# A fused chain of RNN, scan, LSTM and adapted layer: a shorter lead of the RNN, another slot plan, and the input bias on VectorE

## The chip, the cores and the metric

The kernel runs on one core of a Trainium2 chip. The metric is the device time of one execution in microseconds (us), lower is better; the time of a kernel is the median of its runs. A profiled execution has a time of its own, which is given beside its span.

## What is computed

Four layers follow one another, each added to its input. The sequence is 1024 steps long, the batch 4, the width 512; everything is in 32-bit floats. `cond` is one vector per batch row.

```python
# L0, an RNN, started from h0 = cond
next_h = jnp.tanh(x_t @ Wx + b + prev_h @ Wh)
# L1, taps that come from cond, two projections, a linear scan
proj = conv @ Wp + bp;  b_t = softplus(proj[..., :64]);  c_t = tanh(proj[..., 64:]);  u = x @ Ws + bs
state = decay * state + dt * b_t * u_t;   y_t = c_t * state;   out = y @ Wo + bo
# L2, an LSTM, started from h0 = cond, c0 = 0; gates i, f, o (sigmoid) and g (tanh)
A = x_t @ Wx + b + prev_h @ Wh
next_c = f * prev_c + i * g;   next_h = o * jnp.tanh(next_c)
# L3, a weight per batch row, made from cond: layernorm, w1, gelu, w2, then a rank-8 product
layer = base_layer[None] + jnp.einsum('bdr,bkr->bdk', x_a, x_b);   out = einsum('btc,bco->bto', x, layer)
```

L0 and L2 are recurrences: step t needs step t-1 whole. L3's weight depends on `cond` alone, so it is made once.

## The kernel before

**Tiling.** Everything is kept transposed: 128 partitions hold a quarter of the width, 4 such quarters lie side by side, then time, then batch. Time is cut into 32 chunks of 32 steps. Products are cut into four column tiles of 32, which run beside one another on TensorE.

**Stages.** `do_pass(c)` (L712) runs 32 steps. In each step t it issues one LSTM step of chunk c, one RNN step of chunk c+2, and whatever *jobs* stand in that slot: the scan layer of chunk c+1 (`ssm_jobs`, L416), the adapted layer of chunk c-1 (`adapt_jobs`, L661), the RNN's input projection of chunk c+3 (`project0`, L292), the LSTM's input projection of chunk c+1 (`input_jobs`, L689) and its bias (`late_jobs`, L705). So the RNN leads the LSTM by two chunks, 64 steps. Passes -2 and -1 have RNN steps and no LSTM; in passes 30 and 31 the RNN is over.

**Order.** The order is written out by hand; each engine does its instructions in the order of issue. A job is a triple: slot t, a place, and the function. Place "pe" comes after the LSTM's matmuls and ahead of the RNN's; "gap" comes on VectorE and ScalarE after half B's cell and ahead of its h; "end" comes after the RNN's tanh. Within one slot and place the jobs go in the order of the list: adapt, scan, x load, RNN projection, input projection, bias.

**An LSTM step.** The width is dealt with in two halves, A and B, so that one's elementwise work lies beside the other's matmuls. `lstm_mm` (L350) issues 96 matmuls (the state is carried in three 16-bit parts): A with the state of half A, part of B, A with half B's state, the rest of B. Then for each half: a 32 x 32 block transposition out of PSUM (L377), a sum over the parts and the input (L382), the tanh of all gates (L389), products (L393), cell (L398), tanh (L403), h (L406) and two subtractions that split h (L187). The next step's first matmul waits for half A's second split; its half-B matmuls wait for half B's. The input, `xw2`, is copied in by ScalarE one step ahead (`lstm_input`, L366).

**An RNN step.** 32 matmuls (L335), a transposition (L343), a sum (L344), a tanh (L347).

**Input projection.** For each group of 8 steps: four jobs of 8 matmul records (`input_mm`, L316), two transpositions out of PSUM (`input_turn`, L320), then the bias and a scale of 0.5 for three gates, by ScalarE, 32 calls per chunk (`input_bias`, L328). All four groups of chunk c+1 are projected in slots 15 to 30 of pass c.

**Set-up.** `early` (L629) holds functions for given steps of passes -2 to 0, issued after the "end" jobs: the split of the LSTM's weights into 16-bit parts (`split_wh2`, 16 blocks, 3 in 2 of each 3 steps from step 4), the decay, the fold of the convolution's bias (`fold_conv`), centring and norm of `cond` (`adapt_center`, `adapt_norm`), `adapt_hidden`, then 32 blocks of w2 (`adapt_w2`, one per step from slot 3 of pass -1, so 29 in pass -1 and 3 in pass 0), `adapt_gather`, `adapt_sum`, and 16 blocks of the weight (`adapt_layer`, slots 8 to 30 of pass 0). w2 comes in 32 loads of 512 KB through four buffers that reuse the place of the weight; load j+4 is issued by `adapt_w2(j)` (L581, L583). `base_identity` (L618) adds the identity.

**Slots in a steady pass.** RNN projection 0, 10, 11, 12; taps 1 to 4 and the skip product 5; adapted layer's sums 2 to 5, products 6 to 9; elementwise work of the scan layer 4 to 12; its output product 13; input projection 15 to 30; x load (four DMAs of 64 KB on SyncE) 2. No slot has two PE jobs.

Of the kernel before, what the change touches and what calls it, by code (L numbers as in the profile page):

```python
# [14 lines left out]
P = 128  # L15
# [5 lines left out]
TG = 8  # L21
CT = 32
# [15 lines left out]
def cond_resid_kernel(ctx: ExitStack, tc: tile.TileContext, a: dict, out: bass.AP):  # L38

# [135 lines left out]
    def load_late():  # L175
        quads(nc.sync, w1, a["w1"].rearrange("(j c q) n -> j q c n", j=4, c=KC))
        for j in range(W2_BUFS):
            load_w2(j)
        quads(nc.sync, base, a["base"].rearrange("(j c q) n -> j q c n", j=4, c=KC))
# [63 lines left out]
    def prepare_decay():  # L243
        for f in softplus_parts(sp, vec[:NS, 2:4], 2, "p"):
            f()
        nc.vector.tensor_mul(dec1, sp[:, 0:1], dt)
        nc.vector.tensor_scalar(dec1, dec1, -1.0, 1.0, ALU.mult, ALU.add)
        nc.vector.tensor_copy(decay, dec1.to_broadcast([NS, TC]))
# [12 lines left out]
    b2s = const.tile([P, 4, KC], F32, name="b2s", tag="b2s")  # L261

    def scale_b2():
        nc.vector.tensor_scalar(b2s[:, 0:3], b2[:, 0:3], 0.5, None, ALU.mult)
        nc.vector.tensor_copy(b2s[:, 3], b2[:, 3])

    def split_wh2(k, g):

        w, scale, cols = layer[:, k, g], 0.5 if g == 3 else 0.25, slice(g * D, (g + 1) * D)
# [55 lines left out]
    def input_bias(c, n, g, m):  # L325

        x = xw2[c % 2][:, g, m, TG * n : TG * (n + 2), :]
        nc.scalar.activation(x, x, AF.Identity, bias=b2s[:, g, m : m + 1], scale=1.0 if g == 3 else 0.5)  # L328
# [39 lines left out]
    class Half:  # L368
# [19 lines left out]
        def gates(self):  # L388
            nc.scalar.activation(self.gc[:, :4], self.gc[:, :4], AF.Tanh)  # L389
# [26 lines left out]
    def ssm_jobs(c):  # L416
# [3 lines left out]
        def sm(name):  # L420
            return small.tile([NS, TOK], F32, name=name, tag=name, bufs=1)

        jobs = [
            (m // 2, ("gap", "end")[m % 2], lambda m=m: v.tensor_add(x1[:, m, 3:, :], x[:, m], h[:, m]))
            for m in range(KC)
# [22 lines left out]
        jobs += [(1 + k, "pe", lambda k=k: taps(k)) for k in range(KC)]  # L448
        jobs.append((5, "pe", skip))

        def turn(n):
# [5 lines left out]
            (4, "end", lambda: act.activation(z, pb[:NS, 0, :], AF.Identity, bias=vec[:NS, 0:1])),  # L457
            (4, "end", lambda: act.activation(e, pb[:NS, 0, :], AF.Abs, bias=vec[:NS, 0:1])),
            (5, "end", lambda: act.activation(e, e, AF.Exp, scale=-1.0)),
            (5, "end", lambda: act.activation(u, e, AF.Copy, bias=2.0)),  # L460
            (6, "end", lambda: act.activation(cg, pb[NS:, 0, :], AF.Tanh, bias=vec[NS:, 0:1])),
            (7, "end", lambda: v.tensor_mul(u, u, e)),
            (7, "end", lambda: v.tensor_mul(w, u, u)),
            (7, "end", lambda: act.activation(p, w, AF.Copy, scale=2.0 * SERIES[-1])),
            (12, "end", lambda: act.copy(s1, y_last)),
# [17 lines left out]
        jobs += [(6 + n // 3, place(n), lambda n=n: turn(n)) for n in range(4)]  # L483
        jobs += [(8 + n // 3, place(n), f) for n, f in enumerate(chain)]
# [6 lines left out]
        def x2_end(m):  # L491
# [6 lines left out]
            (13, "pe", out_mm),  # L498
            *((13 + m // 2, "end", lambda m=m: x2_end(m)) for m in range(KC)),
            (14, "end", lambda: act.copy(x1[:, :, 0:3, :], x1[:, :, TC : TC + 3, :])),  # L500
# [4 lines left out]
    hid = prep.tile([P, KC, B], F32, name="hid", tag="hid")  # L505
# [45 lines left out]
    def adapt_hidden():  # L551
# [12 lines left out]
        nc.vector.tensor_add(hid, tt[:, :, :B], bm1.unsqueeze(2).to_broadcast([P, KC, B]))  # L564
        nc.scalar.activation(hid, hid, AF.Gelu)

    def adapt_w2(j):
# [4 lines left out]
        for k in range(KC):  # L572
            for t in range(4):
                n0 = P // 2 * (t % 2)
                nc.tensor.matmul(  # L575
                    ps[CT * t : CT * t + B, :], hid[:, k, :], w2[j][:, t // 2, k, n0 : n0 + P // 2],
                    start=(k == 0), stop=(k == KC - 1),
                )
        for t in range(4):
            copy = (nc.vector.tensor_copy, nc.scalar.copy)[t % 2]  # L580
            copy(xr[CT * t : CT * t + B, half, hd, rg], ps[CT * t : CT * t + B, :])  # L581
# [36 lines left out]
    def base_identity():  # L618
# [11 lines left out]
    early = {  # L630
        (-2, 9): [prepare_decay], (-2, 12): [scale_b2], (-2, 24): [fold_conv], (-2, 26): [adapt_center], (-2, 28): [adapt_norm],
        (-1, 2): [adapt_hidden], (-1, 20): [base_identity],
    }
# [3 lines left out]

    late = None
    for n in range(4 * KC):
        first, second = split_wh2((1, 0, 2, 3)[n // 4], n % 4)  # L640
        t = 4 + 3 * n // 2
        if late:
            at(-2, t, late)
        at(-2, t, first)
        late = second
    at(-2, 29, late)
    at(-2, 30, load_late)

    for half in range(2):
        at(-1, half, lambda half=half: adapt_bias(half))  # L650
        at(0, 7, lambda half=half: adapt_sum(half))
    for j in range(NW2):
        c, t = divmod(3 + j, TC)
        at(c - 1, t, lambda j=j: adapt_w2(j))
        if j % (NW2 // 2) == NW2 // 2 - 1:
            at(c - 1, t, lambda half=j // (NW2 // 2): adapt_gather(half))
    for n in range(B * KC):
        at(0, 8 + 3 * n // 2, lambda n=n: adapt_layer(n // KC, n % KC))
# [200 lines left out]
```

## Time and profile before

| | |
|---|---|
| median of 3 runs | 4811.99 us (4811.18 to 4814.89) |
| profiled execution: time, span | 4806.8 us, 4805.0 us |
| first LSTM transposition (L377) | 192.4 us |
| pass 0, from its first LSTM transposition to the next pass's | 162.9 us |
| a pass of 2 to 29, mean of the same | 143.3 us |
| pass 30, the RNN over | 142.5 us |
| TensorE's granted clock, mean | 0.993 |
| TensorE at half clock | 29.9 to 36.7, 43.6 to 50.4, 57.2 to 111.8 us |

How it is read. The page gives for each engine the busy time, its share of the span and the number of instructions; PE is the matmuls, PEld the weight loads, DVE VectorE, ACT ScalarE, POOL GpSimd, SP SyncE. A matmul's record is 0.27 us long while the next one starts some hundredth of a us later, so a matmul group's worth is read from start to start. The chain is the work that ended last, followed back from the end, with each engine's and line's share of the span. In a table of stretches each row has the stretch (us from the start), its length, then the busy time and instructions of PE, PEld, DVE, ACT and POOL, then the granted clock, DMA's share and GB/s. In a timeline each row has the start, the time to the end of the last of the merged instructions, the engine, the line, the operation, what it writes and reads, shapes, how many, and in brackets the idle time before it and what ended it.

### The profile page before, as it was taken

To read this page: it belongs to the slowest core of one execution; us is meant where nothing else is said; L and a number is where in the kernel's file an instruction comes from. 1 tells how busy PE (TensorE), PEld (TensorE's weight loads), DVE (VectorE), ACT (ScalarE), POOL (GpSimd) and SP (SyncE) were. 2 spreads that over 40 slices of the span, in tenths; PEclk is the share of its full clock that TensorE was granted. 3 is DMA by queue.
4 is the path that set the end of the run, shared out by engine and by line. 5 is a ranking of instruction groups with operands and counts; after the bars stand their busy time and mean duration, and the time that the engine had idled before them with its cause. 6 is when DMAs were issued, how large, how long until landed. Compare 5 with 4: busy or idle time off the path is not lost.

```text
span 4805.0 us, 321617 instructions
## 1 busy us (share of the span) xinstructions
PE 4609.9 (96%) x147040; PEld 3529.9 (73%) x147040; DVE 3816.7 (79%) x17843; ACT 1749.1 (36%) x8712; POOL 52.1 (1%) x95
## 2 busy tenths in 40 slices
PE   6899999999999999999999999999999999999876
PEld 4777777777777777777777777777777777777654
DVE  3678888888888888888888888888888878888776
ACT  2333333333333333333333333333333333333332
POOL 2100000000000000000000000000000000000000
PEclk7999999999999999999999999999999999999999
DMA  6400000000000000000000000000000000000000
GB/s 138 130 4 9 9 9 9 7 7 9 9 9 9 7 8 7 9 9 9 7 9 7 9 9 9 7 9 6 9 9 9 9 7 6 9 7 6 6 3 7
DMA packets 38787, 67.47 MB, mean 14 GB/s; under 512 B 9056, under 2 KB 26080, under 8 KB 36400
## 3 DMA queue, kind: packets, MB, share of 16 engines
q1 hardware_dynamic: 34064, 46.68, 3.8%
q8 instruction: 1149, 18.83, 1.7%
q14 instruction: 214, 1.75, 0.1%
q0 software_dynamic: 2208, 0.19, 0.1%
q10 hardware_dynamic: 1152, 0.01, 0.0%
HBM read 38.34 MB, written 8.39 MB: 10 GB/s over the span
## 4 chain that ended last, share of the span: by engine, by line
PE 94%; DVE 5%; issue 1%; ACT 0%; DMA 0%; ACTq 0%; DVEq 0%; SPq 0%
PE acc L360 58%; PE acc L335 18%; PE proj L316 9%; PE pb L290 3%; PE proj L290 2%; PE ada L673 2%; DVE tt L377 1%; DVE gc L382 1%; DVE h L187 1%; PE ssm_out L290 1%; DVE h L406 1%; DVE prod L393 0%; DVE gc L398 0%; PE pl L615 0%; PE pp L575 0%
## 5 line engine op out<-in xcount | busy, mean ns | idle before, releaser
L360 PE MATMUL acc<-wh,h 128*12 128x256 bf16 x98304 | 2875.0, 273 | 134.7 <-DVE h L187 130.0
L360 PEld LDWEIGHTS <-h 128*12 128x12 bf16 x98304 | 2266.7, 87 | 693.9 <-DVE h L187 372.3
L377 DVE STREAM_TRANSPOSE tt<-acc 128x256 f32<-128x256 f32 x2048 | 922.0, 450 | 425.5 <-PE acc L360 305.6
L335 PEld LDWEIGHTS acc<-wh,h 128*4 128x4 f32 x32768 | 815.6, 88 | 521.3 <-issue 212.2
L335 PE MATMUL acc<-wh,h 128*4 128x128 f32 x32768 | 1109.1, 276 | 31.6 <-ACT h L347 27.8
L389 ACT ACTIVATE gc<-gc 128x32 f32<-128x32 f32 x2048 | 469.7, 229 | 1038.6 <-DVE gc L382 948.4
L382 DVE TENSOR_REDUCE gc<-tt 128x32 f32<-128x128 f32 x2048 | 777.1, 379 | 35.3
L187 DVE TENSOR_TENSOR h<-h 128x8 f32<-128x8 f32 (+1 forms) x4098 | 681.1, 166 | 104.7
L403 ACT ACTIVATE th<-gc 128x8 f32<-128x8 f32 x2048 | 427.2, 209 | 831.9 <-DVE gc L398 831.9
L347 ACT ACTIVATE h<-pre 128x16 f32<-128x16 f32 x1024 | 221.4, 216 | 1144.7 <-DVE pre L344 1144.7
L316 PE MATMUL proj<-wx,x 128*32 128x512 f32 x4096 | 529.5, 592 | 2.6 <-issue 1.5
L406 DVE SCALAR_TENSOR_TENSOR h<-gc,th 128x8 f32<-128x8 f32 x2048 | 343.1, 168 | 221.8 <-ACT th L403 205.1
L343 DVE STREAM_TRANSPOSE tt<-acc 128x128 f32<-128x128 f32 x1024 | 316.2, 309 | 70.3 <-PE acc L335 70.1
L398 DVE SCALAR_TENSOR_TENSOR gc<-prod 128x8 f32<-128x8 f32 x2048 | 341.9, 167 | 35.5
L366 ACT COPY tt<-xw 128x32 f32<-128x32 f32 x2048 | 327.9, 207 | 0.0
L393 DVE SCALAR_TENSOR_TENSOR prod<-gc 128x16 f32<-128x16 f32 x2048 | 315.3, 154 | 0.0
L328 ACT ACTIVATE xw<-xw,b2s 128x64 f32<-128x64 f32 x1024 | 293.6, 334 | 0.4
L344 DVE TENSOR_TENSOR pre<-xw,tt 128x16 f32<-128x16 f32 x1024 | 179.8, 176 | 37.4
L290 PE MATMUL proj<-xin,wx 128*32 128x128 f32 x4096 | 138.8, 278 | 11.9 <-DMA wx<-in_Wx_dram 11.8
L290 PE MATMUL pb<-x,wp 128*32 128x128 f32 x4096 | 139.5, 274 | 0.1
L673 PE MATMUL ada<-layer,x 128*32 128x512 f32 x1024 | 131.6, 592 | 3.0 <-DVE x L666 3.0
L290 PEld LDWEIGHTS proj<-xin,wx 128*32 128x32 f32 x4096 | 117.1, 112 | 14.0 <-DMA wh<-in_Wh_dram 11.8
(116 smaller groups left out, 1179.0 us busy)
## 6 DMA issues: line engine op xcount, KB each, us to landing
layer<-in_w2T_dram SPq DMA_DIRECT2D x32, 512.0 KB, 4.1
xin<-in_xT_dram SPq DMA_DIRECT2D x128, 64.0 KB, 2.1
out_dram<-x SPq DMA_DIRECT2D x128, 64.0 KB, 1.8
layer<-in_Wh_dram SPq DMA_DIRECT2D x16, 256.0 KB, 9.7
wx<-in_Wx_dram SPq DMA_DIRECT2D x4, 1024.0 KB, 15.5
wx<-in_Wx_dram SPq DMA_DIRECT2D x4, 256.0 KB, 5.2
wh<-in_Wh_dram SPq DMA_DIRECT2D x4, 256.0 KB, 7.9
layer<-in_w_dram SPq DMA_DIRECT2D x4, 256.0 KB, 23.7
```

The costliest lines, as they stand in the source:

```text
L187: nc.vector.tensor_tensor(h[:, :, n], h[:, :, n - 1], upper(h[:, :, n - 1]), ALU.subtract)
L290: nc.tensor.matmul(dst[CT * j : CT * (j + 1)], columns(j), x, start=first, stop=final)
L316: nc.tensor.matmul(ps[CT * j : CT * (j + 1), :], tok, w[:, j], start=(k == 0), stop=(k == KC - 1))
L335: nc.tensor.matmul(acc0[CT * j : CT * j + B, :], h[:, k, (t - 1) % TC, :], wh0[:, k, j * P : (j + 1) * P], start=(k == 0), stop=(k == KC - 1),
L360: nc.tensor.matmul(acc2[mh][CT * j : CT * j + NP * B, :], parts, w[:, :, n0 : n0 + 2 * CT], start=(k == 0 and n == 0), stop=(k == KC - 1 a ...
L366: nc.scalar.copy(tt2[m][t % 2][:, :, :, :B], xw2[c % 2][:, :, 2 * m : 2 * m + 2, t, :])
L377: nc.vector.transpose(self.tt[:, :, :, B:].rearrange("p g c b -> p (g c) b"), acc2[self.m])
L382: nc.vector.tensor_reduce(self.gc[:, :4].rearrange("p g c b -> p (g c) b"), self.tt[:, :, :, : (1 + NP) * B].rearrange("p g c (s b) -> p ( ...
L389: nc.scalar.activation(self.gc[:, :4], self.gc[:, :4], AF.Tanh)
L398: nc.vector.scalar_tensor_tensor(self.c, self.prod[:, 1], 0.5, self.prod[:, 0], ALU.mult, ALU.add)
L403: nc.scalar.activation(self.th, self.c, AF.Tanh, scale=0.5)
L406: nc.vector.scalar_tensor_tensor(self.out[:, :, 0], self.gc[:, 2], 1.0, self.th, ALU.add, ALU.mult)
```

## The change

The RNN leads by `LEAD` = 52 steps. In pass c and slot t the RNN's step is chunk and step `divmod(c * 32 + t + 52, 32)`; pass -2 starts at slot 12. So chunk c+1's RNN output is complete after slot 11, and the scan layer moves from slots 0 to 14 to slots 9 to 26. Of the LSTM's input projection only the first 8 steps of chunk c+1 are made in pass c (slots 25 to 30); the other three groups are made in the pass that uses them, from slots 0, 4 and 8. One of a group's two transpositions moves from "end" to "gap". The bias is one VectorE addition for two gates (eight per chunk), half of them in an "end" and half in a "gap"; it no longer scales. In its place the weights and the bias of gate g are doubled once and the gates' tanh has a scale of 0.5. The sum of x and h is three VectorE calls, the last on the last four steps. The set-up is numbered by RNN steps: one weight split per step from step 5, w2 blocks from step 32, two in three steps, 12 before the LSTM's first step and 20 in pass 0, each with 32 weight columns in place of 4 and one ScalarE copy in place of four copies; the sums and the identity at steps 23 and 24 of pass 0, the weight's blocks from slot 25 of pass 0 to slot 8 of pass 1, and the adapted layer's products at slots 16 and 21 to 23.

```diff
+LEAD = TC + 20
...
+    def double_g(k):
+        w = wx2[:, k, 3 * D :]
+        nc.scalar.activation(w, w, AF.Copy, scale=2.0)
...
-        w, scale, cols = layer[:, k, g], 0.5 if g == 3 else 0.25, slice(g * D, (g + 1) * D)
+        w, scale, cols = layer[:, k, g], 1.0 if g == 3 else 0.5, slice(g * D, (g + 1) * D)
...
-    def input_bias(c, n, g, m):
-
-        x = xw2[c % 2][:, g, m, TG * n : TG * (n + 2), :]
-        nc.scalar.activation(x, x, AF.Identity, bias=b2s[:, g, m : m + 1], scale=1.0 if g == 3 else 0.5)
+    def input_bias(c, n, g):
+
+        x = xw2[c % 2][:, g : g + 2, :, TG * n : TG * (n + 1), :].rearrange("p g c t b -> p g c (t b)")
+        nc.vector.tensor_add(x, x, b2[:, g : g + 2].unsqueeze(3).to_broadcast([P, 2, KC, TG * B]))
...
-            nc.scalar.activation(self.gc[:, :4], self.gc[:, :4], AF.Tanh)
+            nc.scalar.activation(self.gc[:, :4], self.gc[:, :4], AF.Tanh, scale=0.5)
...
         jobs = [
-            (m // 2, ("gap", "end")[m % 2], lambda m=m: v.tensor_add(x1[:, m, 3:, :], x[:, m], h[:, m]))
-            for m in range(KC)
+            (9, "end", lambda: add(slice(0, 2), 0, TC - 4)),
+            (10, "gap", lambda: add(slice(2, 4), 0, TC - 4)),
+            (11, "end", lambda: add(slice(0, 4), TC - 4, TC)),
         ]
...
-        jobs += [(1 + k, "pe", lambda k=k: taps(k)) for k in range(KC)]
-        jobs.append((5, "pe", skip))
+        jobs += [(12 + k, "pe", lambda k=k: taps(k)) for k in range(KC)]
+        jobs.append((16, "pe", skip))
...
-            (12, "end", lambda: act.copy(s1, y_last)),
+            (23, "end", lambda: act.copy(s1, y_last)),
...
-        jobs += [(6 + n // 3, place(n), lambda n=n: turn(n)) for n in range(4)]
-        jobs += [(8 + n // 3, place(n), f) for n, f in enumerate(chain)]
+        jobs += [(17 + n // 3, place(n), lambda n=n: turn(n)) for n in range(4)]
+        jobs += [(19 + n // 3, place(n), f) for n, f in enumerate(chain)]
...
-            (13, "pe", out_mm),
-            *((13 + m // 2, "end", lambda m=m: x2_end(m)) for m in range(KC)),
+            (24, "pe", out_mm),
+            *((24 + (m + 1) // 2, ("end", "gap")[m % 2], lambda m=m: x2_end(m)) for m in range(KC)),
...
-                    ps[CT * t : CT * t + B, :], hid[:, k, :], w2[j][:, t // 2, k, n0 : n0 + P // 2],
+                    ps[CT * t : CT * (t + 1), :], hid[:, k, :], w2[j][:, t // 2, k, n0 : n0 + P // 2],
...
-        for t in range(4):
-            copy = (nc.vector.tensor_copy, nc.scalar.copy)[t % 2]
-            copy(xr[CT * t : CT * t + B, half, hd, rg], ps[CT * t : CT * t + B, :])
+        nc.scalar.copy(xr[:, half, hd, rg], ps)
...
+    def at_step(i, f):
+
+        c, t = divmod(i - LEAD, TC)
+        at(c, t, f)
+
+    for n, f in enumerate(decay_parts()):
+        at_step(1 + n // 2, f)
...
+            at_step(5 + n, late)
+        at_step(5 + n, first)
...
+    at_step(10, load_w1)
+    for j in range(W2_BUFS):
+        at_step((14, 18)[j // 2], lambda j=j: load_w2(j))
+    at_step(21, load_base)
+    at_step(20, fold_conv)
     for half in range(2):
+        at_step(27 + half, lambda half=half: adapt_bias(half))
+    at_step(24, adapt_center)
+    at_step(25, adapt_norm)
+    at_step(26, lambda: nc.scalar.activation(b2[:, 3], b2[:, 3], AF.Copy, scale=2.0))
+    for k in range(KC):
+        at_step(26 + k, lambda k=k: double_g(k))
+    at_step(30, adapt_hidden)
+    NPRE = 12
     for j in range(NW2):
+        f = lambda j=j: adapt_w2(j)
+        if j < NPRE:
+            at_step(32 + 3 * j // 2, f)
+        else:
+            at(0, j - NPRE, f)
...
+    for half in range(2):
+        at(0, 24, lambda half=half: adapt_sum(half))
+    at(0, 23, base_identity)
     for n in range(B * KC):
-        at(0, 8 + 3 * n // 2, lambda n=n: adapt_layer(n // KC, n % KC))
+        c, t = divmod(25 + n, TC)
+        at(c, t, lambda n=n: adapt_layer(n % B, n // B))
...
-        jobs = [(2 + m, "end", lambda m=m: add(m)) for m in range(KC)]
-        jobs += [(6 + k, "pe", lambda k=k: mm(k)) for k in range(KC)]
-        return jobs + [(5 + KC, "end", end)]
+        jobs = [((1, 2, 5, 6)[m], "end", lambda m=m: add(m)) for m in range(KC)]
+        jobs += [((16, 21, 22, 23)[k], "pe", lambda k=k: mm(k)) for k in range(KC)]
+        return jobs + [(23, "end", end)]
...
+    def input_jobs(c, n, t):
...
+        last = t + KC - 1
+        return [(t + k, "pe", lambda k=k: mm(k)) for k in range(KC)] + [
+            (last, "end", lambda: input_turn(c, n, 0, ps[0])),
+            (last + 1, "gap", lambda: input_turn(c, n, 2, ps[0])),
+            (last + 1, "end", lambda: input_bias(c, n, 0)),
+            (last + 2, "gap", lambda: input_bias(c, n, 2)),
+        ]
...
-            jobs.append((2, "end", lambda: load_x(c + 4, src)))
+            jobs.append((12, "end", lambda: load_x(c + 4, src)))
...
-                t = ((0, 10, 11, 12) if lstm else (8, 10, 12, 14))[m]
-                jobs += [(t, "pe", mm), (t, "end", end)]
+                jobs += [(17 + m, "pe", mm), (17 + m, "end", end)]
...
+            r = divmod(c * TC + t + LEAD, TC)
...
-                rnn_mm(c + 2, t)
+                rnn_mm(*r)
```

## The prediction

> **What bounds the kernel now.** I read the page's busy shares first, then a stretch without the RNN, then one full step.
>
> ```profile
> PE 4609.9 (96%) x147040; PEld 3529.9 (73%) x147040; DVE 3816.7 (79%) x17843; ACT 1749.1 (36%) x8712; POOL 52.1 (1%) x95
> PE acc L360 58%; PE acc L335 18%; PE proj L316 9%; PE pb L290 3%; PE proj L290 2%; PE ada L673 2%; DVE tt L377 1%; DVE gc L382 1%; DVE h L187 1%; PE ssm_out L290 1%; DVE h L406 1%; DVE prod L393 0%; DVE gc L398 0%; PE pl L615 0%; PE pp L575 0%
> ```
>
> This looks bound by TensorE. The stretches say otherwise: pass 0, pass 16, and pass 30, where the RNN is over.
>
> ```profile
> 192.40:355.30 162.90, 157.59 (x4668) 116.31 (x4669) 127.53 (x573) 54.44 (x274) 8.43 (x15) 1.00 0.03 6
> 2507.30:2650.20 142.90, 141.34 (x4572) 108.88 (x4567) 117.43 (x553) 53.47 (x269) 0.00 (x0) 1.00 0.03 8
> 4512.10:4654.70 142.60, 112.06 (x3420) 80.35 (x3416) 104.22 (x489) 45.59 (x233) 0.00 (x0) 1.00 0.02 5
> ```
>
> Pass 30 has 29 us less matmul and takes the same 142.6 us: 32 steps of 4.455 us. The period is the LSTM's own loop. In the timeline of pass 31 the LSTM's 96 matmuls start at 4701.77 and again at 4706.22; the chain of waits there reads 2.82 us matmuls and 1.6 us of VectorE in series. What room is left beside it shows in a steady step with an extra PE job:
>
> ```profile
> 3106.45 1.03 PE L673 MATMUL ada<-layer,x 128*32 128x512 f32 x8
> 3107.30 1.05 PE L335 MATMUL acc<-wh,h 128*4 128x128 f32 x32
> 3108.28 2.79 PE L360 MATMUL acc<-wh,h 128*12 128x256 bf16 x96
> 3110.90 1.03 PE L673 MATMUL ada<-layer,x 128*32 128x512 f32 x8
> 3111.76 1.05 PE L335 MATMUL acc<-wh,h 128*4 128x128 f32 x32
> 3112.73 0.50 PE L360 MATMUL acc<-wh,h 128*12 128x256 bf16 x12
> ```
>
> Start to start: LSTM 2.62, job 0.86, RNN 0.97, of which it needs 0.88 (0.775 from first to last start, plus one group's 0.11). So the loop has 0.09 us free on PE in a step with one job, and no room for a second. VectorE's windows, from the same timeline: between half B's cell and its h it waits for the tanh ("gap"), and a 0.34 us reciprocal at 3108.26 fits there exactly, B's h starting 0.33 us after the LSTM's start as it does without. B's splits then end 0.91 after that start, and PE wants them at 0.98. After the RNN's sum ("end", 1.34 after the start) half A's transposition starts at 1.87 and may slip to 1.99: it did at 3137.01, and half B's still came on time. So: 0.34 us free in a gap, 0.65 us in an end. Before the LSTM starts, a step is 2.02 us at full clock and 2.78 us at half:
>
> ```profile
> 25.49 1.06 PE L335 MATMUL acc<-wh,h 128*4 128x128 f32 x32 [0.97 <-ACT h L347]
> 62.71 1.89 PE L335 MATMUL acc<-wh,h 128*4 128x128 f32 x32 [0.90 <-ACT h L347]
> ```
>
> The clock stood at half from 57.2 to 111.8 us and twice for 6.8 us before. The first A transposition is at 192.4 us; passes 2 to 29 average 143.3 us, 0.8 above 32 x 4.455.
>
> [...] PE shows holes put down to "issue" (0.58 us at 203.85) just after an x load. [...]
>
> **The change, part by part.**
>
> (1) *Set-up, 64 RNN steps to 52.* Steps 0 to 5 as before: step 5 at 28.7 us. Steps 5 to 21 each carry a full Wh2 split: RNN h 0.22, copy 0.60, activation 0.63, VectorE 0.69, then transposition and sum 0.48 in series, some 2.65 us with hand-overs, 2.78 at half clock; the matmul of x (L290, 0.87 us) at steps 5 to 8 lies in PE's idle 0.97 us. 17 x 2.74 + 0.8 for the conv fold (its step took 3.61 for 2.78) = 47.3: 76.0. Two at 2.78 (81.6), centring and norm 3.65 each (88.9; as at 90.55 to 94.22), four at 2.8 (100.1; ScalarE's 0.6 us doubling of wx2 and VectorE's 0.69 us bias copy fit beside them), hidden 3.6, one at 2.4: step 32 at 106.1. Then four steps with taps at 2.5; the twelve from the skip product to the input matmuls took 35.6 us (121.58 to 157.21), less 2 for fewer W2 blocks and no VectorE copies of them; three at 2.15; 2.1 to the first LSTM transposition: 10 + 33.6 + 6.5 + 2.1 = 52. Sum 158 against 192.4: **-34** (bounds -47, clock at full from step 22; -24, all at half). The W1, W2 and base loads go to SP earlier by step number, but SP waits for the splits as before, and DMA is idle by 95 us; the x load (slot 2 to 12) and the output's DMAs (9 to 23) pass nothing that is due on SP.
>
> (2) *Passes 0 and 1.* Twenty W2 blocks now stand in pass 0 instead of three. One needs 0.44 us on PE between starts (174.50 to 174.94[...]), behind a job in a loop with 0.09 left: 20 x 0.48 = 10. Sixteen of the 512 KB loads fall there; after a 256 KB x load, steps 3 to 5 of passes 1 to 29 run 0.32 us over in all on average, so about as much for each, 5 (bounds 0 and 16). The identity (3.1 us of VectorE at 164.26) lies at an end already holding y: 3.1. The two sums of step 24: 1.0 (1.45 at step 7 before); they need POOL's last 16 gather DMAs, 0.57 us each after step 19 and 3.3 to land, done by step 23. Adapted layers: 1.06 us each beside a job (280.52 to 281.58), sixteen before and after: about equal, 14.7. So 33.8 where passes 0 and 1 had 20.3 + 1.3 above normal: **+12** (+3 to +27).
>
> (3) *Steady passes, 1 to 29.* All jobs now stand in other slots; what matters is where they meet.
> - Slot 16 has two PE jobs, adapt's first product (0.86) and the skip product (0.77, 3101.99 to 3102.76): 2.62 + 0.86 + 0.77 + 0.88 = 5.13, +0.68. Behind them wait the RNN and the next LSTM.
> - A 0.443 us input transposition (L320) moves from end to gap at 4, 8, 12, 29: 0.10 over the window, 0.02 absorbed: 4 x 0.085.
> - The bias, 32 ScalarE calls per chunk (0.334 us, hidden) to 8 VectorE ones at 0.42. In the end slot free; in the gap at 5, 9, 13, 30: 4 x 0.06. ScalarE's relief gives nothing: it was not late.
> - Slot 11's end: the sum of x and h waits for the same step's RNN tanh (ends 1.60), 0.22, then a 0.443 transposition: A's transposition at 2.22 for 1.99 allowed, +0.22. All of VectorE's next step queues behind it.
> - Slot 23's end: adapt's 0.585 us copy now goes ahead of the state copy on ScalarE, and y on VectorE waits for that copy: A's transposition at 2.48, +0.49, where the old slot 12 cost 0.15: +0.34.
> - The rest 0.02. Gates with a scale, the doubled weights, the x load at another slot: 0.
>
> Sum 1.84, taken as **1.8 us per pass, 29 x 1.8 = +52** (bounds: 0.7, only PE's double slot; 2.6). Passes 30 and 31: +1.
>
> Sum against the profiled execution: 4806.8 (span 4805.0) - 34 + 12 + 52 + 1 = 4838. The median of the runs is 5.2 above that execution, so **4843**. The cover for the cheap parts is the loop's slack; if it is gone, each gap job costs its whole 0.42 us.
>
> **Rivals.**
> *Slack takes the slips (not slower).* One mechanism: half B's h and half A's transposition have more room than I read, so no VectorE or ScalarE slip reaches PE, and only slot 16 costs, 0.68 x 29 = 20. For: no steady step but 12, 13 and those with holes exceeds 4.46. Against: the 3108.28 step leaves 0.07 us. 4812 - 34 + 12 + 20 + 1 = 4811. It decides below 0.72 us a pass, (34 - 12 - 1)/29.
> *Clock stays up in the set-up.* [...] up to ten steps at 0.76 and the split steps at 0.13 less, of which I count 9: 4834. Against: fold and norm products didn't lift it at 84 to 98 us.
> *Loads starve PE in pass 0, and gap jobs cost more.* W2 loads 0.9 us each (16 x 0.6 = +10), the eight gap slips 0.08 more each (8 x 0.08 x 29 = +18): 4871. For: the holes at 203.85. Against: DMA's share in pass -1 is higher, and few holes show there.
> *It doesn't start earlier*: set-up data not there at step 52. A W2 block is asked for every 3.5 us, and its load takes 4.1 with four in flight, so the last input product would have to be late, by one step of 2.2 at least: 4845.
>
> **Chances.** Forecast 0.44 (own range 4826 to 4862), slack 0.20 (half of it ends faster, if the set-up also gains more), clock 0.15, starved 0.19, no earlier start 0.02. Low end 4808, high 4870 leave out 2 in 10. Measurement tells 0.2% (9.6 us) from no change: faster 0.09, same 0.11, slower 0.80.
>
> **What will show it.** First A transposition near 158 us; pass 0 near 167; a steady pass near 145.1 with step 16 at 5.13, step 24 near 4.95, slips of 0.06 to 0.1 behind slots 4, 5, 8, 9, 12, 13, 29, 30. Wrong if step 16 stays below 4.6, or the first transposition comes before 146 or after 168.

## The result, and the profile after

| | before | after |
|---|---|---|
| median of the runs, us | 4810.14 (4804.76 to 4814.89, 11 runs) | 4823.21 (4819.36 to 4830.07, 11 runs) |
| profiled execution: time, span, us | 4806.8, 4805.0 | 4822.1, 4820.3 |
| first LSTM transposition (L377, now L379), us | 192.4 | 162.15 |
| pass 0, pass 1, us | 162.9, 144.7 | 169.2, 154.2 |
| a pass of 2 to 29, mean, us | 143.3 | 144.3 |
| pass 30, us | 142.5 | 142.6 |
| TensorE at half clock, us | 29.9 to 36.7, 43.6 to 50.4, 57.2 to 111.8 | 39.4 to 42.9, 46.3 to 100.9, 292.0 to 295.4 |

The ratio of after to before is 1.003 (95% interval 1.002 to 1.0039): slower, by 13 us. The forecast was slower by 31 us (4843 against the 4812 known then). The direction was right; the loss is some four tenths of the one forecast.

The page of the changed kernel, busy shares and the chain's shares by line:

```profile
PE 4609.6 (96%) x147040; PEld 3536.0 (73%) x147040; DVE 3864.6 (80%) x18001; ACT 1494.4 (31%) x7661; POOL 53.5 (1%) x96
PE acc L362 57%; PE acc L337 16%; PE proj L318 9%; PE pb L292 3%; PE proj L292 2%; DVE tt L379 2%; PE ada L702 2%; DVE gc L384 1%; DVE h L191 1%; DVE h L408 1%; DVE prod L395 1%; DVE gc L400 1%; DVE tt L345 0%; ACT x L709 0%; PE pl L624 0%
```

ScalarE lost 255 us of busy time and VectorE gained 48. Neither number shows in the time: as before, the page says little, and the stretches of pass 0, pass 16 and pass 30 have to be read.

```profile
162.15:331.31 169.16, 157.93 (x5193) 129.72 (x5184) 126.40 (x580) 47.21 (x256) 18.02 (x32) 0.99 0.18 56
2504.52:2648.71 144.19, 141.70 (x4570) 108.87 (x4561) 119.31 (x559) 45.78 (x237) 0.00 (x0) 1.00 0.03 8
4525.65:4668.27 142.62, 121.54 (x3803) 89.55 (x3795) 110.95 (x520) 40.34 (x213) 0.00 (x0) 1.00 0.02 5
```

Pass 30 stands where it stood, although the RNN's last 12 steps now fall into it (121.5 for 112.1 us busy on TensorE) and it has both new kinds of VectorE jobs in its gaps. Pass 16 takes 1.4 us more than before (144.2 for 142.8 from transposition to transposition), for the same work on TensorE. So what costs there is where jobs meet, not how much there is. From start to start of half A's transposition the 32 steps of a pass can be compared one by one; the medians over passes 1 to 29, less 4.455 us, are zero but for these:

| step | before | after | forecast for the new slot |
|---|---|---|---|
| 16 (two PE jobs) | no such step | +0.77 | +0.68 |
| 11 and 12 (the last sum of x and h) | 0 | +0.28, -0.18 | +0.22 |
| 23 and 24 (old 12, 13; the output's copy) | +0.16 net | +0.66, -0.18 (+0.48 net) | +0.49 |
| 4, 5, 8, 9, 12, 13, 29, 30 (jobs in the gap) | 0 | 0.00 | 0.58 together |

The sum of the medians is 1.37 us a pass after and 0.23 before. The mean pass lost 1.0: scattered holes of TensorE put down to "issue" took about 0.1 less a pass than before.

Step 16 in the timeline of TensorE, the counterpart of the one-job step shown before:

```profile
3151.53 2.79 PE L362 MATMUL acc<-wh,h 128*12 128x256 bf16 x96
3154.15 1.03 PE L702 MATMUL ada<-layer,x 128*32 128x512 f32 x8
3155.01 0.93 PE L292 MATMUL pb<-x,ws 128*32 128x128 f32 x14
...
3155.78 1.03 PE L337 MATMUL acc<-wh,h 128*4 128x128 f32 x28
...
3156.66 2.77 PE L362 MATMUL acc<-wh,h 128*12 128x256 bf16 x92
```

LSTM 2.62, first job 0.86, second 0.77, RNN 0.88: 5.13 from LSTM to LSTM, which is the forecast's own sum. The LSTM step after it takes 4.55 (to 3161.21), another 0.09 over the usual 4.46, and the two make the 0.77 of the table.

The gap, in VectorE's timeline: cell, job, half B's h, in a step with a bias; below it the same two in a step without a job.

```profile
3106.55 0.17 DVE L400 SCALAR_TENSOR_TENSOR gc<-prod 128x8 f32<-128x8 f32 x1
3106.64 0.42 DVE L330 TENSOR_TENSOR xw<-xw,b 128x256 f32<-128x256 f32 x1
3107.00 0.17 DVE L408 SCALAR_TENSOR_TENSOR h<-gc,th 128x8 f32<-128x8 f32 x1
```

```profile
3133.28 0.17 DVE L400 SCALAR_TENSOR_TENSOR gc<-prod 128x8 f32<-128x8 f32 x1
3133.73 0.17 DVE L408 SCALAR_TENSOR_TENSOR h<-gc,th 128x8 f32<-128x8 f32 x1 [0.28 <-ACT th L405]
```

From cell to h it is 0.45 us both times. The bias's record is 0.42 us long and yet the h starts 0.36 after the bias does: the records of successive VectorE operations overlap. This is where the forecast went wrong.

The set-up, as stretches between changes of the granted clock, and the two longest holes in TensorE's timeline (in brackets the idle time and what it is put down to), with one RNN step at half clock:

```profile
15.55:39.43 23.88, 12.74 (x404) 10.07 (x400) 6.49 (x28) 4.40 (x15) 11.53 (x24) 1.00 0.98 198
...
46.27:100.87 54.60, 41.37 (x628) 25.04 (x632) 28.55 (x77) 21.10 (x50) 6.89 (x10) 0.50 0.62 144
100.88:162.15 61.27, 45.11 (x1578) 37.21 (x1569) 21.45 (x83) 13.55 (x55) 0.00 (x0) 1.00 0.34 110
```

```profile
29.95 0.28 PE L337 MATMUL acc<-wh,h 128*4 128x128 f32 x2 [2.35 <-issue]
...
39.16 0.28 PE L337 MATMUL acc<-wh,h 128*4 128x128 f32 x2 [4.65 <-issue]
```

The holes stand in the middle of an RNN step's 32 matmuls, where TensorE waits for no other engine, while DMA's share is 0.98. What comes just before their end stands below, with the run without the load of x. Before, the longest hole of this kind in the set-up was 1.9 us.

### The profile page after: what moved, and what is told of

The parts are those of the page before. It is cut to its first block, busy times and chain, and to the rows that moved or that the text cites. A ratio compares the mean times of both kernels' runs of the same rounds, so it can differ in the third digit from the quotient of the medians.

```text
span 4820.3 us, 320719 instructions
## 1 busy us (share of the span) xinstructions
PE 4609.6 (96%) x147040; PEld 3536.0 (73%) x147040; DVE 3864.6 (80%) x18001; ACT 1494.4 (31%) x7661; POOL 53.5 (1%) x96
## 3 DMA queue, kind: packets, MB, share of 16 engines
q8 instruction: 1149, 18.83, 1.6%
## 4 chain that ended last, share of the span: by engine, by line
PE 89%; DVE 8%; issue 1%; ACT 1%; DMA 0%; ACTq 0%; SPq 0%; DVEq 0%
PE acc L362 57%; PE acc L337 16%; PE proj L318 9%; PE pb L292 3%; PE proj L292 2%; DVE tt L379 2%; PE ada L702 2%; DVE gc L384 1%; DVE h L191 1%; DVE h L408 1%; DVE prod L395 1%; DVE gc L400 1%; DVE tt L345 0%; ACT x L709 0%; PE pl L624 0%
## 5 line engine op out<-in xcount | busy, mean ns | idle before, releaser
L379 DVE STREAM_TRANSPOSE tt<-acc 128x256 f32<-128x256 f32 x2048 | 918.8, 449 | 453.0 <-PE acc L362 334.9
L318 PEld LDWEIGHTS proj<-wx,x 128*32 128x32 f32 x4096 | 118.0, 110 | 6.2 <-DVE x L500 0.7
```

The costliest lines, as they stand in the source:

```text
L318: nc.tensor.matmul(ps[CT * j : CT * (j + 1), :], tok, w[:, j], start=(k == 0), stop=(k == KC - 1))
L379: nc.vector.transpose(self.tt[:, :, :, B:].rearrange("p g c b -> p (g c) b"), acc2[self.m])
```

## The experiments

The theory: a step costs what its latest path costs, on TensorE (two jobs), on ScalarE with VectorE behind it (the copy), while a VectorE job counts from its start to the next one's start, not by its whole record. The rival is the forecast's reading, in which the gap holds 0.34 us of record. All twelve kernels are the changed one with the edit shown, unless it says otherwise, so they are compared with 4823 us, ratio 1.003. Ratios are to the kernel before, timed beside each; medians of kernels that were timed in different groups can be compared to a few us at best.

### One extra product a step at most

```diff
-        jobs += [((16, 21, 22, 23)[k], "pe", lambda k=k: mm(k)) for k in range(KC)]
+        jobs += [((20, 21, 22, 23)[k], "pe", lambda k=k: mm(k)) for k in range(KC)]
...
-                jobs += [(17 + m, "pe", mm), (17 + m, "end", end)]
+                t = (17, 18, 19, 29)[m]
+                jobs += [(t, "pe", mm), (t, "end", end)]
```

> The changed kernel with adapt's first product at slot 20 instead of 16 and the RNN projection's last quarter at slot 29 instead of 20, so that no slot has two PE jobs. Theory (two products in slot 16 make that step 0.77 us longer, since PE has 0.09 us free beside one job): steps 16 of passes 1 to 29 fall from 5.22 to 4.46, 29 x 0.77 = 22 us off the changed kernel's 4823, some 4801. Rival (the long step comes from the skip product's wait for ScalarE's reading of the same PSUM tile, which stays in slot 16): step 16 stays near 5.2 and the time near 4823.

Measured: 4803.32 us (4800.14 to 4807.26), ratio 0.9991 (0.9983 to 0.9999). Step 16 is back at 4.46; the other steps keep what they had. Its TensorE timeline:

```profile
3141.84 2.79 PE L362 MATMUL acc<-wh,h 128*12 128x256 bf16 x96
3144.47 0.93 PE L292 MATMUL pb<-x,ws 128*32 128x128 f32 x14
...
3145.24 1.14 PE L337 MATMUL acc<-wh,h 128*4 128x128 f32 x30
3146.30 2.80 PE L362 MATMUL acc<-wh,h 128*12 128x256 bf16 x96
```

4.46 from LSTM to LSTM with the skip product alone. The same number of matmuls, elsewhere, is worth 16 to 20 us: 20 between the two medians, 19 by the ratios, 16 when each kernel is set against the kernel before that was timed beside it. This step of the forecast held.

### The output's copy one slot later

```diff
-        return jobs + [(23, "end", end)]
+        return jobs + [(24, "end", end)]
```

> The changed kernel with adapt's PSUM copy and output DMAs at the end of slot 24 instead of 23, so that ScalarE's state copy, and y on VectorE behind it, no longer queue behind a 0.59 us copy. Theory (ScalarE's order): the two steps 23 and 24 together fall from +0.48 to the +0.16 that the kernel before had at its slots 12 and 13, 29 x 0.32 = 9 us off, some 4814. Rival (the +0.48 is the output product waiting for y on PE, whatever stands ahead of the state copy): no change, 4823.

Measured: 4812.75 us (4805.15 to 4823.88), ratio 1.0015 (1.0008 to 1.0022). Steps 23 and 24 went from +0.66 and -0.18 to +0.11 and +0.03. In the changed kernel, ScalarE's timeline at the end of slot 23 has the output's copy ahead of the state's copy:

```profile
3189.49 0.58 ACT L709 COPY x<-ada 128x512 f32<-128x512 f32 x1
3189.97 0.19 ACT L473 COPY s<-w 64x4 f32<-64x4 f32 x1
```

and VectorE's timeline of the same steps, y with its wait, then half A's transposition:

```profile
3190.20 0.34 DVE L488 SCALAR_TENSOR_TENSOR w<-w,sp,cg 64x128 f32<-64x128 f32 x1 [0.90 <-ACT s L473]
3190.47 0.43 DVE L379 STREAM_TRANSPOSE tt<-acc 128x256 f32<-128x256 f32 x1
```

With the copy a slot later, y's wait is less than half:

```profile
3186.68 0.34 DVE L488 SCALAR_TENSOR_TENSOR w<-w,sp,cg 64x128 f32<-64x128 f32 x1 [0.37 <-ACT s L473]
3186.95 0.43 DVE L379 STREAM_TRANSPOSE tt<-acc 128x256 f32<-128x256 f32 x1
```

A 0.58 us copy on an engine that is busy 31% of the span cost 7 us (by the ratios and by the kernels timed beside) to 10 us (between the medians), because VectorE's queue stood behind it. This step of the forecast held as well.

### Both biases in one gap

```diff
-            (last + 1, "end", lambda: input_bias(c, n, 0)),
+            (last + 2, "gap", lambda: input_bias(c, n, 0)),
```

> The changed kernel with both bias additions of a group in one gap (slots 30, 5, 9, 13) and none in the end. Theory of the gap (an operation takes its duration less an overlap of about 0.08 us with the next, so 0.35 us of gap takes one 0.42 us addition free, and a second one costs its whole start-to-start time): each of the four steps grows by 0.30 to 0.34, 4 x 29 x 0.32 = 37 us, some 4860. The prediction's reading (0.34 us free, whole durations count) would have had one at +0.06 and two at +0.48. Rival (PE doesn't wait for half B's h at all within a step, so that gap jobs cost nothing): 4823.

Measured: 4856.09 us (4852.63 to 4859.56), ratio 1.0103 (1.0089 to 1.0117). Steps 5, 9 and 13 rose by 0.29, step 30 by 0.27. VectorE's timeline in such a step:

```profile
3131.93 0.17 DVE L400 SCALAR_TENSOR_TENSOR gc<-prod 128x8 f32<-128x8 f32 x1
3132.01 0.75 DVE L330 TENSOR_TENSOR xw<-xw,b 128x256 f32<-128x256 f32 x2
3132.68 0.15 DVE L408 SCALAR_TENSOR_TENSOR h<-gc,th 128x8 f32<-128x8 f32 x1
```

Two additions of 0.42 us take 0.75 together, so the second starts 0.33 after the first; the h comes 0.75 after the cell instead of 0.45, and these 0.30 reach the step nearly whole. From the first job's start to the h there are 0.37 us without a delay (0.45 less 0.08), and one addition takes 0.33 of them. So the gap is about as tight as the forecast thought; its error was to count the job by its record. The first bias is free, the second is not.

### No bias

The two lines of `input_jobs` that issue the bias are left out, and with them the bias term of the output.

```diff
-            (last + 1, "end", lambda: input_bias(c, n, 0)),
-            (last + 2, "gap", lambda: input_bias(c, n, 2)),
```

> Leaves out both additions of the LSTM's bias (the output lacks that term), so the transpositions' gap at the RNN transposition's slots stays but no 0.42 us addition runs in any gap or at any step's end. My theory since the second experiment set (successive VectorE operations overlap by 0.07 to 0.08 us, so a job of 0.42 us fits into the gap): no change, 4823 within 3 us. The prediction's reading (the gap holds 0.34 us, each addition in a gap slips by 0.06 and the one at a step's end is free): 29 passes x 4 x 0.06 = 7 us faster, 4816.

Measured: 4827.05 us (4824.78 to 4828.55), ratio 1.0037 (1.0024 to 1.0049): no gain, and 1 us more than the theory allowed. The sum of the steps' medians is 1.40 us, with the bias 1.37. Eight VectorE additions a pass cost nothing where they stand. (The set-up of the profiled execution was 165.6 us long, 3.5 more than that of the changed kernel. In the nine executions with the changed kernel's lead, loads and blocks it lies between 160.8 and 165.6, so 3 us of set-up in one execution tell nothing.)

### The RNN's lead back to 64

```diff
-LEAD = TC + 20
+LEAD = TC + 32
```

> The changed kernel with LEAD = 64: one constant, the slot plan and the set-up by RNN steps as they are. Theory (a RNN-only step costs its latency, and the LSTM's loop hides the rest): twelve more steps of some 2.02 to 2.2 us ahead of the LSTM, the first LSTM transposition at 186 to 188 instead of 162, +25 us, some 4848; the steady passes unchanged. Rival (the lead is worth nothing, since PE has the same work in all): 4823.

Measured: 4842.9 us (4841.77 to 4843.08), ratio 1.0075 (1.0063 to 1.0088). The first LSTM transposition is at 186.1 instead of 162.15: twelve RNN steps at 2.0 us. The passes are as they were but for steps 11 and 12, whose wait is gone, since the hidden state that the last sum needs is then twelve steps old. So the shorter lead itself saved 24 us in the set-up and cost about 3 in the passes; what the change did beside it gave back more than that.

### The transposition ahead of the last sum

Only in slot 11 and place "end" the two jobs change places.

```diff
-            for slot, where, f in jobs:
+            for slot, where, f in jobs[::-1] if (t, place) == (11, "end") else jobs:
```

> At the end of slot 11 alone, the LSTM input's transposition (0.44 us) is issued ahead of the last sum x+h (0.23 us), which waits 0.28 us there for the RNN's tanh. My theory: the transposition then runs inside that wait, the next half's accumulator transposition is no longer late, and the +0.10 us of steps 11 and 12 goes: 29 x 0.10 = 3 us faster, 4820. Rival (the wait itself is what costs, whatever runs inside it: the sum still ends after the tanh, so the next half is still late by nearly the sum's 0.23 us): no change or slightly slower, 4823 to 4826.

Measured: 4827.94 us (4822.83 to 4831.19), ratio 1.0039 (1.0026 to 1.0053). The steps did what the theory says and the time did not follow. VectorE's timeline of the changed kernel, then of this one:

```profile
3135.02 0.23 DVE L427 TENSOR_TENSOR x<-xin,h 128x64 f32<-128x64 f32 x1 [0.28 <-ACT h L349]
3135.16 0.44 DVE L322 STREAM_TRANSPOSE xw<-proj 128x256 f32<-128x256 f32 x1
3135.52 0.41 DVE L379 STREAM_TRANSPOSE tt<-acc 128x256 f32<-128x256 f32 x1
```

```profile
3142.69 0.44 DVE L322 STREAM_TRANSPOSE xw<-proj 128x256 f32<-128x256 f32 x1
3143.06 0.22 DVE L427 TENSOR_TENSOR x<-xin,h 128x64 f32<-128x64 f32 x1
3143.29 0.45 DVE L379 STREAM_TRANSPOSE tt<-acc 128x256 f32<-128x256 f32 x1
```

The idle 0.28 is filled and half A's transposition is on time; steps 11 and 12 have medians of 0.00 in place of +0.28 and -0.18. That is worth 0.10 x 29 = 3 us. But the scattered holes took 17.1 us in this execution and 10.1 in that of the changed kernel (steps of passes 2 to 29 that are more than 0.1 over their slot's median, their excess summed). In the fourteen profiled executions of this study, that sum lies between 9.1 and 18.8. A gain of 3 us can be seen in the steps and not in the time.

### Both single edits

The copy one slot later and one extra product a step at most, as above.

> The edits of the first two experiments together: one extra matrix product a step at most (the adaptation's first product from slot 16 to slot 20, the RNN input's last one from slot 20 to slot 29), and the copy of the output one slot later (24). My theory: both work on different steps, so the savings add: 4823 - 20 - 10.5 = 4793, some 17 us below the kernel before. Rival (step 24 has the output projection's product; with the first product of the adaptation moved into slot 20, the last one stays in 23 and its end, now waited for at the end of 24, runs into another queue): only the 20 us of the first edit, 4803.

Measured: 4795.44 us (4792.9 to 4803.64), ratio 0.9973 (0.9963 to 0.9983). The savings add. The sum of the medians is 0.34 us a pass. This is the change's shorter lead without its two collisions, and it is faster than the kernel before.

### More of TensorE in the set-up

```diff
+    idle_ps = bank("idle", [P, TOK], tag="po", bufs=1)
+
+    def busy(n):
+        for i in range(n):
+            tiled(idle_ps, lambda j: wx0[:, i % KC, P * j : P * j + CT], xin[0][:, i % KC])
+
+    for i in range(4, 31):
+        at_step(i, lambda: busy(5))
```

> At the end of RNN steps 4 to 30 of the set-up, 20 matmuls of 32x128 columns whose result nobody reads, about 0.6 us at full clock: they run while VectorE and ScalarE form the next hidden state. Theory A (the granted clock was halved from 46 to 101 us because TensorE had too little to do there; steps took 2.78 us at half and 2.02 us at full clock): the clock stays full, some 19 steps get shorter by up to 0.76 us, set-up 8 to 14 us shorter, 4809 to 4815. Theory B (the pace of these steps is that of the loads, or the clock is halved for another reason): no gain; at half clock the 20 matmuls take 1.2 us and make each step longer by about 0.3 us, 8 us slower, 4831.

Measured: 4842.07 us (4835.97 to 4844.72), ratio 1.0067 (1.0055 to 1.008). The first transposition is at 179.4, 17 us later. In this execution the clock was full from 78.5 us on, with TensorE busy for 19.3 of the next 21.5 us, where the changed kernel ran at half until 100.9. Yet the steps with a weight split only went from 2.78 to 2.52 us, not to 2.02. VectorE's timeline shows why, at full clock:

```profile
84.41 0.68 DVE L277 SCALAR_TENSOR_TENSOR xw<-layer,wh 128x512 f32<-128x512 f32 x1
85.01 0.31 DVE L345 STREAM_TRANSPOSE tt<-acc 128x128 f32<-128x128 f32 x1
```

The RNN's matmuls had ended at 84.37 by their record; their transposition stood behind the split's 0.68 us. And TensorE's waits in the set-up grew, here in its table of waits (total us, times, longest), with its own extra matmuls first:

```profile
PE idle L292 <- issue: 11.9, 5, 5.7
PE acc L337 <- issue: 9.5, 3, 5.8
```

21 us of such holes, for 7.0 in the changed kernel: 14 of the 17 us. With 1080 matmul records more, while DMA's share was 1.00 from 16 to 40 us and 0.85 and 0.71 in the next two stretches of 20, TensorE had more holes. Neither theory was right as a whole: the clock was full earlier, that was worth 0.26 us in a split step, and most of the price was the holes.

### More blocks in the set-up

```diff
-    NPRE = 12
+    NPRE = 20
...
-            at_step(32 + 3 * j // 2, f)
+            at_step(32 + j, f)
```

The gather of the first half moves with its last block.

> 20 blocks of the adaptation's second weight projected in the set-up instead of 12, one an RNN step from step 32 instead of two in three steps, and 12 instead of 20 in pass 0. Theory: a block's 32 matmuls (0.63 us as a row, about 0.45 of TensorE's time) lie in pass 0 on the path and in the set-up beside the hidden state's VectorE and ScalarE work; 8 x 0.45 = 4 us off pass 0, set-up unchanged: 4819. Rival (the blocks' loads, four buffers, don't keep up with one block an RNN step of 2.02 us, and TensorE waits in the set-up for each): set-up longer by more than the 4 us, 4825 to 4835.

Measured: 4824.14 us (4819.5 to 4828.39), ratio 1.0026 (1.0018 to 1.0035). Pass 0 fell by 5.7 us to 163.5, 0.7 for each of the eight blocks; the set-up rose by 3.3 to 165.4. No wait for a w2 load shows on TensorE, so the rival's mechanism is not there. What shows are three holes at the blocks' matmuls:

```profile
PE pp L586 <- issue: 3.1, 3, 2.0
```

The longest of them, at 119.2 us, stands where the changed kernel has one of 1.4 us at other matmuls (118.7). So the forecast's 0.73 us for a block in pass 0 (0.48, an estimate, and a share of the loads) was about right; on TensorE a block in pass 0 of the changed kernel takes 0.45 us from start to start (189.37 to 189.82). Whether the set-up pays for the move is open: 165.4 us lies within the spread of set-ups given above, and the time can't tell a gain of the forecast's 4 us from none.

### No load of x in the steady passes

x is loaded for the first four chunks only, and the later ones are computed from their values.

```diff
-        if src is not None:
+        if src is not None and c < 0:
```

> Leaves out the load of x in passes 0 to 27 (four transfers of 64 KB each pass, at slot 12); those chunks are computed from the first chunks' x. Theory (the scattered holes put down to issue in slots 14, 15 and 17 to 21 of some passes, 0.37 us a pass on average apart from pass 1's layers, come while this load or what it sends back stands in front of TensorE's instructions): the holes go, some 10 us faster, 4813. Rival (they come with the stream of instructions, whatever the load): no change, 4823 within 4 us.

Measured: 4831.7 us (4825.42 to 4834.01), ratio 1.0036 (1.0023 to 1.0049): nothing gained. (The median is 9 us above the rival's 4823, by the ratio it is 3.) The scattered holes are still there, 14.2 us, nearly all in slots 14 to 21 as in the changed kernel. The theory fell, and the hole just after an x load that the prediction named is no evidence that the load made it.

The traces show what comes just before the end of these holes. The page lists a DMA queue that carries instructions (packets, MB, share of 16 engines):

```profile
q8 instruction: 1149, 18.83, 1.6%
```

18.83 MB in 1149 packets is 16 KB for each, and over TensorE's 294,080 matmuls and weight loads it is 64 bytes for each. So, as an estimate from these counts, a packet holds 256 of TensorE's instructions; with the extra matmuls in the set-up there were 1157 packets. The traces of all fourteen kernels have 461 holes of over 0.15 us on TensorE put down to issue after the first 16 us. Of these, 453 end 1.20 to 1.65 us after such a packet landed; moments picked at random between 200 and 4600 us in the changed kernel's trace lie 0.2 to 4.0 us after one (nine in ten of them). So these holes are read as TensorE's waits for its own instructions. The hole that ends at 39.16 began at 34.51, its packet moved from 36.51 to 37.84.

In the steady passes the long steps follow where instructions are dense. In the changed kernel slots 13 to 20 issue 311 to 321 matmuls and weight loads each, most others 272 or fewer, and all steps counted as holes lie in slots 14 to 21. Before, slots 0 to 4 and 10 to 13 were the dense ones, and the long steps lie in slots 0, 2 to 5 and 11 to 14. With 320 in a step of 4.455 us, 256 are used up in 3.56 us; between the starts of two packets it is 3.75 us in slots 14 to 20 (median). That the packets just fail to keep up there is the author's estimate from these two numbers: no run varies the density alone, so it is not shown.

### All three edits

The copy, the products and the order in slot 11.

> The three edits that took time off single steps together: one extra product a step at most, the output's copy one slot later, and in slot 11 the input's transposition ahead of the last sum. Theory: they add, medians of the steps' excess near 0.25 us a pass instead of 1.37; 4795 - 3 = 4792. Rival: the third edit brings nothing beside the others, as it did not show in the time by itself: 4795.

Measured: 4798.4 us (4794.97 to 4802.6), ratio 0.997 (0.9958 to 0.9982), the same as with two edits within the intervals. Steps 11 and 12 are at 0.00 again; the scattered holes took 18.8 us in this execution and 16.0 with two edits. The third edit can't be told from none by the time.

### Later loads in the set-up

The kernel with both single edits, and:

```diff
-    for c in (1, 0, 2, 3):
+    def load_wh2(c):
         quads(nc.sync, layer[:, c], ...)
+    load_wh2(1)
+    load_wh2(0)
...
-    wx2 = load_rows(const, "wx2", a["Wx2"], 4 * D, nc.sync)
+    wx2 = const.tile([P, KC, 4 * D], F32, name="wx2", tag="wx2")
...
+    at_step(6, lambda: load_wh2(2))
+    at_step(7, lambda: load_wh2(3))
+    at_step(9, lambda: quads(nc.sync, wx2, ...))
```

> The kernel with both single edits (one extra product a step at most; the output's copy one slot later), and in the set-up two of the four quarters of the LSTM's recurrent weight loaded at RNN steps 6 and 7, and its input weight at step 9, instead of all at the start. Theory (the two holes of TensorE put down to issue, 2.35 us before 29.95 and 4.65 us before 39.16 in the changed kernel's profile, come because its instructions wait behind the loads that keep the engines full): with less than full engines at these steps the holes shrink to below 1 us together, the first LSTM transposition comes 5 to 7 us earlier than 161.1, 4788 to 4790. Rival (the loads stand elsewhere and the holes move with them, and a quarter that comes late holds up its conversion): first transposition at 161 to 167, 4795 to 4801.

Measured: 4788.48 us (4782.34 to 4792.82), ratio 0.9956 (0.9942 to 0.9969). The first transposition is at 155.96, for 161.09 without this edit: 5.1 us earlier. TensorE's waits in the set-up, first with both single edits, then with the loads moved (its lines stand two lower):

```profile
PE acc L337 <- issue: 6.6, 2, 4.9
```

```profile
PE acc L339 <- issue: 1.8, 2, 1.3
```

The holes went from 6.6 to 1.8 us. Their sum alone is no safe measure: in the nine executions with the loads unmoved it lies between 2.4 and 7.0, and where it was small, steps before it had run at half clock. But RNN step 8, the first one clear of the holes, starts at 40.0 to 42.2 us in all nine and at 35.2 here, so the gain is there by then. The instruction packets show the same: the second one in this stretch starts at 36.27 with both single edits and at 30.95 here. The rest of the two executions' difference is pass to pass: fewer scattered holes in this one, which the edit doesn't touch. This is the fastest version of the study, 0.4% below the kernel before.

## Why the prediction was wrong, point by point

In the profiled executions the forecast had +31 us and measured +15.3.

| term | forecast | measured | |
|---|---|---|---|
| set-up | -34 | -30.3 | 192.42 to 162.15 |
| passes 0 and 1, above a steady pass | +12 | +14.9 | 6.3 + 9.6 - 1.0 of the steady part |
| steady passes, 1 to 29 | +52 | +29 | 1.0 in each |
| passes 30 and 31 | +1 | +1.8 | |

The last 4 of the 20 us between forecast and result are in how the median stands to the profiled execution: the forecast added 5.2 us, and in the runs made with the result the median stood 3.3 above it before and 1.1 after.

**The step that failed** is the room in the gap: "0.34 us free in a gap", and with it the terms "4 x 0.085" for the moved transpositions and "4 x 0.06" for the biases, 0.58 us a pass or 17 of the 23 us by which the steady passes came out cheaper than forecast. They measured 0.00. The prediction took the 0.34 us of a reciprocal's record as the room and compared other records with it. What counts is from start to start: 0.33 us for a bias with another behind it, 0.36 for a transposition with the next one behind it (slot 11), in a room of 0.37. In the traces the records of these operations overlap the next one's: by 0.06 us a bias with the h behind it (a 0.42 us record, the h 0.36 after its start), by 0.08 the transposition of slot 11 with the next (0.44 and 0.36), by 0.09 two biases (0.42 and 0.33). What the overlap consists of is not shown. The 0.42 us that the forecast gave the bias was an estimate, and the trace has the same 0.42; what was wrong is how it was counted. The experiment with both biases shows that the room is really no larger, and the one without bias that it was enough for the bias. The moved transpositions had no run of their own; that they cost nothing is read from their steps.

**A smaller miss** was in slot 11: the wait's place and cause were right (0.28 us for the RNN's tanh), its price was put at 0.22 us and measured 0.10, since the next step gave 0.18 of the 0.28 back. Half A's transposition was late by 0.28 us, half B's, which followed it without the usual pause, by 0.04.

**Right, with its size:** slot 16 (0.68 forecast, 0.77 measured, 16 to 20 us by experiment), slot 23 (0.34 net forecast, 0.48 - 0.16 = 0.32 measured, 7 to 10 us by experiment), the bias in an "end" slot and the relief of ScalarE (0).

**Passes 0 and 1.** The sum came near (+12 for +14.9), in part by luck: its 5 us for the loads of w2 rest on the steps after an x load, whose holes the load does not make: without it they were still there (14.2 us, for 10.1 in the changed kernel).

**Set-up.** The sum was 158.3 us and 162.15 came. The steps were as forecast, 2.78 at half clock with a split and 2.02 at full clock without. The two holes of 2.35 and 4.65 us were not in the sum: at step 22 the set-up was 7.0 us behind it (83.0 for 76.0), and the terms after step 26 came out 3.2 shorter than forecast. In the last experiment, with later loads, the holes were 1.8 us for 6.6, and step 8 started at 35.2 for 40.0 to 42.2. The long stretch of half clock lasted 54.6 us as before, so the rival in which it stays up fell; in the split steps it would have been worth 0.26 us each, where the rival had 0.13. The clock also changed in shorter pieces than the prediction's 6.8 us: 3.41 us at half from 39.44 to 42.85.

**The rivals.** "Slack takes the slips" had the gap's zero right by luck: its mechanism, more room behind half B's h, is not there, since 0.30 us more in the gap cost 0.27 to 0.29. It was wrong for the two waits of slots 11 and 23, and the time lies between its 4811 and the forecast. "Gap jobs cost more" fell with the gap's terms, and no sign of a late start was seen.

## What to carry to other kernels

Read the cost of short operations from start to start, in a queue where they follow one another, and not from the length of their records: here the difference of 0.08 us decided between 17 us and nothing. In a loop with no slack, count jobs by the step they fall in: two matmul jobs in one slot cost 16 to 20 us and a copy at the wrong end of ScalarE's queue 7 to 10, and moving each by a slot or a few was free. While bulk loads filled the DMA engines (a share of 0.98), TensorE stood idle for up to 4.65 us at a stretch, put down to "issue"; issuing three of the loads later brought the first LSTM transposition 5.1 us forward, so it is worth trying not to issue such loads before they are needed. For such a stretch, look whether a packet of the instruction queue landed just before its end: here 453 of 461 did, 1.20 to 1.65 us before.

## What the runs showed of the hardware

- Two VectorE additions of 256 elements, each 0.42 us by its record, take 0.75 us one after the other: 0.33 from start to start.
- Holes of TensorE put down to "issue" reached 4.65 us at a DMA share of 0.98 in the set-up, and 5.8 us with 1080 matmul records added. 453 of 461 such holes end 1.20 to 1.65 us after a packet of the instruction queue landed, which holds 256 of TensorE's instructions by the estimate above. With the added matmuls four packets of the set-up start 9.3 to 10.4 us after the one before, where it is 3.4 to 4.6 in the steady passes. That the loads hold the packets up is supported by the run with later loads, in which the packet started at 30.95 for 36.27 us and the first LSTM transposition came at 155.96 for 161.09.
- The scattered holes of steady passes, 9 to 19 us in an execution, came with and without the load of x, nearly all at or just behind slots with more than 300 matmuls and weight loads. They set the limit below which a change of a few us can be read only from the steps.
